# Two steps of a gated recurrence read their input products from a shared block instead of computing them alone

## The chip, the cores and the metric

The kernel runs on one core of one Trainium2 chip. The metric is device time of the whole program in microseconds (us), the median of several executions. One execution was recorded by the hardware profiler; every duration below comes from that record, and times "at 838.95" are us from the start of its span.

## What is computed

Two layers with residual connections over x of 64 sequences x 128 steps x 512 features, all in fp32. The first layer is a gated linear recurrence that the kernel does with scans along time. The second is a GRU whose gates also see a conditioning vector. Cut to the second layer:

```
x  = x + layer0(x, cond)                    # scans, no step-by-step matmuls
xz, xr, xh = x @ W_z, x @ W_r, x @ W        # "products of x", 512 -> 3 x 512
vz, vr, vh = cond @ C_z + b_z, cond @ C_r + b_r, cond @ C + b
for t in range(128):                        # h: 64 x 512
    z  = sigmoid(xz[t] + h @ U_z + vz)
    r  = sigmoid(xr[t] + h @ U_r + vr)
    hh = tanh(xh[t] + (r * h) @ U + vh)
    h  = (1 - z) * h + z * hh
out = x + h of every step
```

## The kernel before

**Two halves of the program.** From the start to about 708 us the first layer runs, in 16 groups of 4 sequences. From there the GRU runs. Only the GRU is touched by the change.

**Two streams.** The 64 sequences are split into stream 0 and stream 1 of 32 sequences each. Their steps alternate on the engines, so that one stream's matmuls run while the other stream's vector work is done. Stream 0 starts four steps earlier; stream 1 takes two steps in a row at three places (`CATCH_UP`, line 1099). Below, s0 t10 is step 10 of stream 0. The list `order` fixes the turns; turn 7 is s1 t0, turn 8 is s0 t4, turn 17 is s0 t8, turn 19 is s0 t9, turn 20 is s1 t7, turn 21 is s0 t10, turn 22 is s1 t8, turn 23 is s0 t11, turn 27 is s0 t13.

**One step on the engines** (`Stream.halves`). TensorE (PE) takes 16 matmuls of 256 columns, the r and z gates, h times U (the group `g<-w_s,h`, line 374). ScalarE (ACT) takes the sigmoid of r (L815) and of z (L824). VectorE (DVE) multiplies r and h and transposes the result in two halves (L819, L820). PE takes 16 matmuls of 128 columns with it (`g<-w_s,f`). ACT takes the tanh (L854), DVE makes the new h and transposes it (L866, L867, L871). GpSimd (POOL) makes (1-z)h (L830, L831) and adds x to the output (L882). [...]

**Where the products of x come from.** They must stand in the PSUM bank `g` of the stream before the step's gates are added to it. There are two ways.

- *Direct.* For steps for which `direct` (line 730) is true, ACT copies the conditioning part into the bank (`put_v`, line 777) and PE adds 16 matmuls of 384 columns (`x_products`, the group `g<-w_x,x`). They are issued as filler in the next turn, between that turn's gates and its second matmul. Before the change stream 0 does so up to step 11, stream 1 up to step 7.
- *Shared.* Steps are also put in groups of 8 (a group covers steps 8g to 8g+7 of both streams). The products of a whole group are made by a two-level fast matrix multiplication (7 outer x 7 inner = 49 products, class `Outer`), each product 4 matmuls of 384 columns (line 500). Group 0 is not made so; group 1 covers steps 8 to 15, for all 64 sequences. Sums of the left operands are made on POOL (L708), copies between banks on ACT (L513, L524), reads into the accumulators on DVE (L597, L602), two further adds on DVE (L617) and POOL (L622). A finished block of two steps goes to DRAM (L630, `shares<-W`); a stream loads the rows of its step (`load_share`, L761) into a tile `xz` if the step is even, and into the tile `whole_v`, which held the conditioning part, if it is odd. ACT puts them in the bank (`put_share`, L767) in place of `put_v`.

A block of steps 8 to 11 is finished by the outer product number 5 of the group (after 35 of its 49 products), a block of steps 12 to 15 by the last ones. `load_share` asserts that the stores of its rows have been issued.

**The pace of the products.** `GOALS` (line 1107) is a list of points (turn, number of products placed); `goal` (line 1112) interpolates between them, and each turn calls `place` twice, after its gates and after its second matmul. `place` (line 714) issues products until the number is reached, but it stops when the next product needs a bank copy from a product of the same outer product that it has issued in the same call. So an outer product's seven products go out over three or four calls, and three calls bring seven products at most. Every product is followed by its reads on DVE and by sums on POOL in program order. All matmuls are issued in the order in which the program writes them.

Of the kernel before, what the change touches and what calls it, by code (L numbers as in the profile page):

```python
# [18 lines left out]
def kernel(  # L19
# [39 lines left out]
    B, S, D = x.shape  # L59
# [5 lines left out]
    TW = 8  # L65
# [298 lines left out]
    NX = S // TW  # L364
# [364 lines left out]

    def direct(st, t):  # L730

        return t < (12 if st.s == 0 else 8)

    class Stream:
        def __init__(self, s):
# [54 lines left out]
        def halves(self, t, filler=None, between=None, targets=lambda: (0, 0), busy=False, reads=(4, 0)):  # L790
# [16 lines left out]
            if t + 1 < S and not direct(self, t + 1) and t + 1 not in self.shares:  # L807
                self.load_share(t + 1)
# [46 lines left out]
            if t + 1 < S and not direct(self, t + 1):  # L855
                self.put_share(t + 1)
# [44 lines left out]
            if t + 2 < S and not direct(self, t + 2) and all((t + 2, q) in stored for q in range(Q)):  # L901
                self.load_share(t + 2)
# [182 lines left out]
    for n in range(2):  # L1085
        t = work.tile([P, 5, 3, P], F32, tag="xt", bufs=2, name=f"w_inner{n}")
# [14 lines left out]
    for t in range(LEAD + 1, S):  # L1101
# [3 lines left out]
    at_of = {step_: FIRST + n for n, step_ in enumerate(order)}  # L1105

    GOALS = (
        (8, 0), (17, 35), (27, 81), (at_of[0, S - TW] - 7, 7 * 7 * (NX - 1) - 14),
        (at_of[0, S - TH] - 5, 7 * 7 * (NX - 1)),
    )  # L1110

# [106 lines left out]
```

## Time and profile before

| what | us |
|---|---|
| median of 3 runs | 1927.61 (1926.23 to 1927.84) |
| the profiled execution | 1927.34 |
| its span on the core | 1925.6 |
| PE busy in the span | 1903.3 |
| DVE, POOL, ACT busy | 1547.2, 838.9, 683.9 |
| `g<-w_x,x`, 640 matmul records (20 blocks of 32) | 55.4 |
| end of the last `g<-w_x,x` block | 855 |
| mean granted PE clock | 0.999 |

A busy time is the union of an engine's instructions; PE instructions overlap in the pipeline, so a block of matmuls is timed here from its first start to the next block's first start. "Idle before" is the time in which an engine stood still ahead of a group, and the arrow names the instruction whose end released it. A chain of waits follows the last instruction back through what released it.

### The profile page before, as it was taken

To read this page: it belongs to the slowest core of one execution; us is meant where nothing else is said; L and a number is where in the kernel's file an instruction comes from. 1 tells how busy PE (TensorE), PEld (TensorE's weight loads), DVE (VectorE), ACT (ScalarE), POOL (GpSimd) and SP (SyncE) were. 2 spreads that over 40 slices of the span, in tenths; PEclk is the share of its full clock that TensorE was granted. 3 is DMA by queue.
4 is the path that set the end of the run, shared out by engine and by line. 5 is a ranking of instruction groups with operands and counts; after the bars stand their busy time and mean duration, and the time that the engine had idled before them with its cause. 6 is when DMAs were issued, how large, how long until landed. Compare 5 with 4: busy or idle time off the path is not lost.

```text
span 1925.6 us, 62747 instructions
## 1 busy us (share of the span) xinstructions
PE 1903.3 (99%) x25225; PEld 1107.7 (58%) x25225; DVE 1547.2 (80%) x3382; ACT 683.9 (36%) x1880; POOL 838.9 (44%) x1542
## 2 busy tenths in 40 slices
PE   9999999999999999999999999999999999999998
PEld 5444444444444445666666666666666666666667
DVE  6899999999999996557777777777777777777776
ACT  3122221212122113234444444444444444444434
POOL 1222223222222325345565655655665655655650
PEclk9999999999999999999999999999999999999999
DMA  6642222222222231233343443443443443443343
GB/s 170 162 93 50 49 44 45 60 49 50 54 47 52 38 66 46 53 95 98 107 133 99 119 130 104 116 131 100 126 122 108 124 122 102 134 117 101 113 110 76
DMA packets 276899, 178.90 MB, mean 93 GB/s; under 512 B 159028, under 2 KB 254528, under 8 KB 276608
## 3 DMA queue, kind: packets, MB, share of 16 engines
q1 hardware_dynamic: 276104, 174.81, 35.6%
q8 instruction: 199, 3.26, 0.7%
q14 instruction: 92, 0.75, 0.1%
q10 hardware_dynamic: 504, 0.07, 0.0%
HBM read 93.58 MB, written 81.13 MB: 91 GB/s over the span
## 4 chain that ended last, share of the span: by engine, by line
PE 65%; DVE 32%; issue 2%; DMA 1%; ACT 0%; POOL 0%; DVEq 0%; ACTq 0%; SPq 0%; POOLq 0%
PE g L374 35%; PE r L500 14%; DVE h L268 10%; PE p L189 4%; DVE h L317 4%; DVE i L300 4%; PE r12a L500 4%; PE shared L500 3%; PE r12b L500 3%; DVE h L307 3%; DVE i L299 2%; DVE i L312 2%; DVE f L284 2%; DVE i L287 2%; DVE h L267 2%
## 5 line engine op out<-in xcount | busy, mean ns | idle before, releaser
L189 PE MATMUL p<-xT,W 128*128 128x512 f32 (+1 forms) x1560 | 670.1, 586 | 1.8 <-ACT xT L148 1.7
L189 PEld LDWEIGHTS p<-xT,W 128*128 128x128 f32 x1560 | 289.6, 190 | 344.2 <-issue 335.9
L374 PE MATMUL g<-w_s,h 128*32 128x256 f32 (+1 forms) x8128 | 481.7, 373 | 3.8 <-DVE h L871 2.1
L374 PEld LDWEIGHTS g<-w_s,h 128*32 128x32 f32 x8128 | 312.6, 110 | 168.3 <-issue 79.0
L374 PEld LDWEIGHTS g<-w_s,f 128*32 128x32 f32 x8128 | 224.5, 109 | 113.2 <-issue 52.1
L374 PE MATMUL g<-w_s,f 128*32 128x128 f32 x8128 | 276.3, 273 | 6.7 <-DVE f L819 5.4
L819 DVE TENSOR_TENSOR f<-f,h 128x64 f32<-128x64 f32 (+1 forms) x494 | 110.7, 224 | 190.5 <-ACT f L815 189.9
L272 POOL COPY first<-condT 128x4 f32<-128x4 f32 x64 | 12.3, 192 | 515.6 <-DVE h L267 501.0
L882 POOL TENSOR_TENSOR h<-h,x 128x128 f32<-128x128 f32 x242 | 123.5, 510 | 237.5 <-DVE h L871 223.5
L268 DVE RECIPROCAL h<-h 128x517 f32<-128x517 f32 x64 | 217.0, 3391 | 2.2
L286 ACT ACTIVATE f<-f 128x512 f32<-128x512 f32 x64 | 40.4, 631 | 461.9 <-DVE f L284 461.9
L815 ACT ACTIVATE f<-g 128x128 f32<-128x128 f32 x254 | 70.6, 278 | 330.7 <-PE g L374 314.4
L830 POOL TENSOR_SCALAR f<-f 128x128 f32<-128x128 f32 x240 | 72.6, 302 | 255.6 <-DVE f L819 248.0
L602 DVE TENSOR_TENSOR W<-r,W 128x384 f32<-128x384 f32 x315 | 170.1, 540 | 9.8 <-PE r L500 0.6
L854 ACT ACTIVATE h<-g 128x128 f32<-128x128 f32 x256 | 71.2, 278 | 242.8 <-PE g L374 242.8
L820 DVE STREAM_TRANSPOSE f<-f 128x64 f32<-128x64 f32 (+1 forms) x494 | 122.2, 247 | 22.5
L866 DVE TENSOR_TENSOR h<-h,f 128x128 f32<-128x128 f32 (+1 forms) x264 | 82.4, 312 | 61.1 <-ACT h L854 61.0
L831 POOL TENSOR_TENSOR f<-f,h 128x128 f32<-128x128 f32 x240 | 112.2, 467 | 20.0
L867 DVE TENSOR_TENSOR h<-h,f 128x128 f32<-128x128 f32 (+1 forms) x264 | 91.9, 348 | 25.8
L210 POOL TENSOR_TENSOR x<-xT,h 128x512 f32<-128x512 f32 x63 | 95.9, 1523 | 4.9
L300 DVE TENSOR_TENSOR_SCAN i<-i,f 128x517 f32<-128x517 f32 x64 | 79.1, 1236 | 6.9 <-ACT i L247 0.5
L317 DVE TENSOR_TENSOR_SCAN h<-f,first 128x517 f32<-128x517 f32 x64 | 79.1, 1236 | 6.5
(167 smaller groups left out, 2790.6 us busy)
## 6 DMA issues: line engine op xcount, KB each, us to landing
shares<-W SPq DMA_DIRECT2D x240, 192.0 KB, 2.0
xz<-shares SPq DMA_DIRECT2D x472, 48.0 KB, 1.9
whole_v<-shares SPq DMA_DIRECT2D x472, 48.0 KB, 1.9
x<-in_x_dram SPq DMA_DIRECT2D x64, 256.0 KB, 4.2
x2d<-x SPq DMA_DIRECT2D x63, 256.0 KB, 3.6
out_dram<-o SPq DMA_DIRECT2D x240, 64.0 KB, 1.8
xw_None<-x2d SPq DMA_DIRECT2D x56, 256.0 KB, 3.4
w_rows<-in_L_cond_W_f_dram SPq DMA_DIRECT2D x4, 256.0 KB, 5.4
```

The source lines that it names most:

```text
L189: nc.tensor.matmul(p[:, tokens], lhsT=W0[:, c, n, k, :], rhs=xT[g][:, k, tokens], start=(k == 0), stop=(k == K - 1),)
L210: nc.gpsimd.tensor_tensor(x2.rearrange("p (t b) -> p t b", b=GB)[:, ts], xT[g][:, c, :].rearrange("p (t b) -> p t b", b=GB)[:, ts], by_bat ...
L268: pin(nc.vector.reciprocal(h, h))
L300: pin(nc.vector.tensor_tensor_scan(i, i, f, 0.0, ALU.add, ALU.mult))
L317: pin(nc.vector.tensor_tensor_scan(h, fs[c % 2], first, 0.0, ALU.mult, ALU.add))
L374: nc.tensor.matmul(p[q * SB : (q + 1) * SB], lhsT=lhsT(k), rhs=part(wk, q), start=(start and k == 0), stop=(stop and k == len(w) - 1), ski ...
L500: nc.tensor.matmul(self.bank(bank)[q * SB : (q + 1) * SB], lhsT=a[:, q * SB : (q + 1) * SB], rhs=w_, start=start, stop=True, skip_group_ch ...
L602: pin(nc.vector.tensor_tensor(dst, r, other, ALU.add))
L819: pin(nc.vector.tensor_tensor(rh[:, e], r[:, e], h_[:, e], ALU.mult))
L820: pin(nc.vector.transpose(rhT[:, e], rh[:, e]))
L831: pin(nc.gpsimd.tensor_tensor(r, r, h_, ALU.mult))
L882: nc.gpsimd.tensor_tensor(hh.rearrange("p (k b) -> p k b", b=SB), hT.rearrange("p (k b) -> p k b", b=SB), x_of(self, t), ALU.add,)
```

## The change

`direct` becomes false for s0 t10 and s0 t11. Stream 0 then computes the products of x by themselves up to step 9, and loads steps 10 and 11 from the shared block. The second point of `GOALS` asks for all 49 products of group 1 by turn 17, where it asked for 35. The third point (81 products by turn 27) and the later ones stay.

```diff
     def direct(st, t):
 
-        return t < (12 if st.s == 0 else 8)
+        return t < (10 if st.s == 0 else 8)
...
     GOALS = (
-        (8, 0), (17, 35), (27, 81), (at_of[0, S - TW] - 7, 7 * 7 * (NX - 1) - 14),
+        (8, 0), (17, 49), (27, 81), (at_of[0, S - TW] - 7, 7 * 7 * (NX - 1) - 14),
         (at_of[0, S - TH] - 5, 7 * 7 * (NX - 1)),
     )
```

## The prediction

> **What bounds the kernel now.** I read the page first for the busiest engine, then the busy times by stage of the GRU, then the timeline of PE around the two blocks that go. The page's first line of engines, the stages (columns: stretch, length, then busy time of PE, PEld, DVE, ACT and POOL, granted clock, DMA share, GB/s) and PE from 837 to 857 us:
>
> ```profile
> PE 1903.3 (99%) x25225; PEld 1107.7 (58%) x25225; DVE 1547.2 (80%) x3382; ACT 683.9 (36%) x1880; POOL 838.9 (44%) x1542
> ```
>
> ```profile
> 736.00:846.00 110.00, 109.86 (x1808) 65.67 (x1812) 62.85 (x177) 36.24 (x112) 45.08 (x90) 1.00 0.24 63
> 846.00:915.00 69.00, 69.00 (x1272) 43.82 (x1268) 50.38 (x152) 30.53 (x92) 39.06 (x79) 1.00 0.35 100
> 915.00:1000.00 85.00, 83.24 (x1596) 53.66 (x1592) 63.03 (x196) 36.84 (x111) 49.05 (x100) 1.00 0.43 118
> 1000.00:1400.00 400.00, 400.00 (x7720) 259.03 (x7714) 297.34 (x948) 180.71 (x543) 230.70 (x480) 1.00 0.42 116
> ```
>
> ```profile
> 838.95 2.79 PE L374 MATMUL g<-w_x,x 128*32 128x384 f32 x32
> 841.53 1.08 PE L374 MATMUL g<-w_s,f 128*32 128x128 f32 x32
> 842.40 0.86 PE L500 MATMUL r12b<-w_inner,inner_sum 128*32 128x384 f32 x8
> 843.05 0.86 PE L500 MATMUL r<-w_x,x 128*32 128x384 f32 x8
> 843.69 1.94 PE L374 MATMUL g<-w_s,h 128*32 128x256 f32 x32
> ...
> 852.54 2.79 PE L374 MATMUL g<-w_x,x 128*32 128x384 f32 x32
> 855.12 1.08 PE L374 MATMUL g<-w_s,f 128*32 128x128 f32 x32
> ```
>
> The reader is to see that PE has no idle time between 736 and 915 us but 0.14 us, while DVE has 57% and 73% of those stretches and POOL 41% and 57%; and that no PE row carries a wait in brackets. A busy PE could hide small gaps, since a block's modelled end overlaps the next block's start by about 0.21 us. So I checked by starts: a block of x products costs 841.53 - 838.95 = 2.58 us, a gates block (h) 845.42 - 843.69 = 1.73, an f block 842.40 - 841.53 = 0.87, a two-level product 843.05 - 842.40 = 0.645. Laying PE's blocks end to end with these four numbers from s0 t4 (742.17) gives the start of s0 t15's gates at 898.72, and the timeline has 898.72. There is not one gap of 0.1 us in 156 us. PE's own work sets the time here, and from 1000 on the stage shows the same.
>
> **The change, part by part.**
>
> *Removed.* The x products of s0 t10 (838.95) and s0 t11 (852.54): 2 x 16 matmuls, 2 x 2.58 = 5.16 us of PE. Both lie in the gapless stretch, so nothing of them is beside other work of PE.
>
> *Kept.* All 49 products of group 1 are made for 64 sequences whether or not stream 0 uses them, so the shared way costs PE nothing more. ACT's copy into the bank is 0.48 us either way (L777 at 848.16 and L767 at 862.39): 0. In the instruction order of the changed kernel, 81 products are placed ahead of s0 t13 as before, and from about there on the order is the same on all five queues but for tile numbers.
>
> *Moved.* The two goals together let products run at the most that the copy rule allows, 7 in three calls, until turn 18. Laid end to end with the same four numbers, the changed order gives:
>
> | start of gates | before | changed | difference |
> |---|---|---|---|
> | s0 t5 | 757.69 | 758.33 | +0.64 |
> | s0 t7 | 796.49 | 799.07 | +2.58 |
> | s0 t9 | 827.53 | 832.04 | +4.51 |
> | s0 t10 | 843.69 | 845.63 | +1.94 |
> | s0 t11 | 857.28 | 856.63 | -0.65 |
> | s0 t13 | 879.93 | 874.77 | -5.16 |
>
> Product 35 starts 5.2 us sooner (805.54 for 810.72), product 49 6.9 sooner (830.11 for 837.02, so in turn 18 and not by 17). A moved product takes along its DVE reads (0.56 each), its ACT copies (0.46 to 0.51) and POOL sums (0.46, or two of 0.72 for an outer sum). A turn in this phase lasts 7.8 to 8.4 us where x products are in it; DVE's busiest such turn before, with the weight differences in it, is 6.7 us (749.93 to 757.69). The changed order there is the same; its fullest later turn, s0 t8, has seven reads and adds of about 0.55 beside the step's own 2.1, so 6.0 of 8.4. I take 0, with 0.5 (one read in the way) as the upper end. No product overtakes a weight difference that it needs: the last one is made at 789.62 before, and product 49, the only one to use it, starts at 830.11.
>
> *Shorter cover.* Where an x block stood between a turn's gates and its f block, only products stand there now. Six turns (s0 t10 to s1 t10) get two products, 1.29 us; before, three of these had that. What must fit in: sigmoid, multiply, transpose. At s1 t9 before, gates' issue ended at 864.83, the first transposed half was ready at 865.97 (DVE L820 ends: 865.73 + 0.25) and the second at 866.37; f started at 866.12, without a gap, since the second half is first needed 0.43 later. So 1.29 is just enough with DVE free. The one visible gap in the run before, at 901.83 after two products, is 0.1. Nearest row for six such turns: 6 x 0.1 = 0.6 at most, likely 0.1. The other end is when POOL works beside DVE; s1 t8 before, from the timeline:
>
> ```profile
> 851.48 1.42 POOL L708 TENSOR_TENSOR sum<-x,sum 128x256 f32<-128x256 f32 x2
> ...
> 851.88 0.41 DVE L819 TENSOR_TENSOR f<-f,h 128x64 f32<-128x64 f32 x1 [1.56 <-ACT f L815]
> 852.33 0.25 DVE L820 STREAM_TRANSPOSE f<-f 128x64 f32<-128x64 f32 x1
> 852.50 0.49 DVE L819 TENSOR_TENSOR f<-f,h 128x64 f32<-128x64 f32 x1
> ```
>
> The multiplies take 0.41 and 0.49 here, beside 0.23 and 0.18 at s1 t9. The second half is ready at 853.27, 2.02 us after the gates' issue: with two products as cover f would be up to 0.73 us late. Here an x block hid it, and the change takes this block away. In the changed order these POOL sums fall in s0 t9 (still with an x block) and s1 t7 (three products), so I take 0.1 and keep 6 x 0.73 = 4.4 as the far end. The Trainium skill (GPSIMD Engine Reference, section Specifications) says that GpSimd's SBUF interfaces are shared with VectorE and contend with instructions of two SBUF inputs, as the multiply is; the two rows above agree. By that rule denser sums speak against the change: stretched at every one of the six turns, the sum would be -0.8 instead of -5.1 (the rival "cover" below).
>
> *Added: eight loads and a wait.* SyncE (SP) issues 4 loads for t10 and 4 for t11, about 0.45 us each (four took 1.79 at 851.90), 3.6 us on a queue that is idle for most of 797 to 862. ACT's `put_share` now waits for them, and behind it stand the next turn's copies and sigmoids, so all of PE. Its due time by the table: the tanh of s0 t9 starts 0.27 after the f block's issue (842.67 against 842.40 before) and the copy 0.31 later, so 838.51 + 0.58 = 839.1. When do the rows come? In the changed order the last two loads of t10 stand behind nine stores on SP, the eighth of which waits for POOL's first late add (L622), in s0 t8. At s0 t9 before, that add ended 5.3 us after the gates' start (832.8 against 827.53); so about 815.23 + 5.3 = 820.5, plus 2.0 for the stores and 1.9 for the loads to land (the page's medians), plus four issues, 1.8: 826.2. That is 12.9 us to spare. In the run before, the analogous load for s1 t8 was issued at 821.80 and used at 842.98:
>
> ```profile
> 821.80 0.31 SPq L761 DMA_DIRECT2D xz<-shares  x1
> ```
>
> ```profile
> 842.98 0.48 ACT L767 COPY g<-xz 128x384 f32<-128x384 f32 x1
> ```
>
> t11 is due about 850 and its last load stands behind the fourth late DVE add or POOL's second add, a turn later (about 835 landed). The tile `xz` for t12 is freed by `put_share` of s1 t8 at about 845 and due at about 861. Cost 0.
>
> *What is late next.* The next wait on the chain is at 919.17, 1.37 us before s1's second step in a row, for DVE (L871). It hangs on that turn's own f block, not on a clock of its own, so it moves along and stays.
>
> **Sum.** -5.16 + 0.1 = -5.1 on the profiled execution's own 1927.34 us: 1922.2. The median before is 0.27 above this execution, so 1922.5 for a median. That is 0.26% faster; a change of under 0.2% (3.9 us) can hardly be told from none here.
>
> **The rivals.**
>
> - *As summed*: 1922.5, between 1921.7 and 1923.7 (0 to 1.1 us given back, by 0.5 of DVE and 0.6 of covers, and the spread of the runs before). For it: the gapless tally. Chance 74%.
> - *Cover*: the shorter covers and denser POOL and DVE work open gaps on PE, 1.2 to 4.4 us in all: 1923.7 to 1926.9. For it: the stretched multiplies. Against: 1000 to 1400 runs at 4.5 us a turn on such covers with PE at 400.00 of 400.00. 12%.
> - *Late rows, slower*: the loads of t10 come behind a later add than I read. In the run before, POOL's four adds end a turn apart, 823 to 848, about 8.2 us each. Behind the fourth and not the first, the rows would land at 826.2 + 3 x 8.2 = 850.8, 11.7 us after 839.1; net +6.6, so 1934.2. It takes time from a landing after 839.1, and loses on balance from 844.2. Against: the order on SP. 5%.
> - *Nothing*: a wait after 877 that does not hang on PE takes up the gain: 1927.6. For it: the rows of later groups also pass DRAM. Against: their stores wait for reads of PE's products, so they move along. 4%.
> - *More*: the wait of 1.37 us at 919 goes as well, because DVE has less left over there: -6.5, 1921.1. 5%.
>
> **How the numbers follow.** The likeliest is 1922.5. The range goes from *more* (1921.1) up into the middle of *cover*, 1925.2; left out are the upper part of *cover*, *late rows* and *nothing*, together some 14%. Faster by over 0.2% (below 1923.75): nearly all of *as summed* and *more*, 0.77. Within 0.2%: *cover*, *nothing* and the edge of *as summed*, 0.18. Slower: 0.05.
>
> **What would show it.** In the changed profile: 576 records of `g<-w_x,x` instead of 640, the last ones in s1 t7; gates of s0 t9 about 4.5 us later and of s0 t13 5.2 us earlier than before; no bracketed wait of PE between 736 and 910; L767 for t10 about 839 right behind its tanh; and the wait of 1.4 us at about 914. A PE gap ahead of `g<-w_s,f` between 845 and 880 would show *cover*; ACT waiting at L767 for `xz<-shares` near 839 or 850 would show *late rows*. The forecast is wrong if some other engine's backlog after 840 reaches PE, which the busy shares do not exclude turn by turn.

## The result, and the profile after

The changed kernel takes **1919.99 us**, the median of 8 executions (1918.50 to 1921.87), against 1926.38 for the kernel before, the median of 8 (1924.65 to 1927.84), the three known before the prediction among them. The ratio is 0.9971, 95% interval 0.9961 to 0.9981: faster by 0.29%. A second comparison, on another occasion, gave 1922.83 (1920.59 to 1924.18, 7 executions) against 1926.90 (23 executions): 0.9975, interval 0.9964 to 0.9987. The forecast was 1922.5 on a level of 1927.61, a ratio of 0.9974. So the forecast ratio lies in both intervals; the absolute number was 2.5 us too high for the first comparison and 0.3 too low for the second, and the first lies below the low end of the range, 1921.1. The profiled execution took 1920.00 us, its span is 1918.0.

The page's first line of engines, then the stages of the GRU (the same columns as for before; the limits are shifted by what PE gained):

```profile
PE 1897.5 (99%) x25161; PEld 1100.3 (57%) x25161; DVE 1544.2 (81%) x3382; ACT 683.5 (36%) x1880; POOL 837.4 (44%) x1542
```

```profile
736.00:846.00 110.00, 109.79 (x1800) 59.45 (x1796) 65.07 (x179) 37.05 (x112) 49.35 (x96) 1.00 0.25 68
846.00:908.00 62.00, 61.95 (x1184) 39.77 (x1180) 46.66 (x146) 28.41 (x86) 32.98 (x71) 1.00 0.37 106
908.00:995.00 87.00, 85.27 (x1634) 55.25 (x1628) 63.79 (x199) 37.56 (x114) 50.65 (x104) 1.00 0.42 115
995.00:1395.00 400.00, 400.00 (x7724) 261.44 (x7717) 296.14 (x948) 180.73 (x543) 230.04 (x480) 1.00 0.42 116
```

PE has 64 instructions less (25225 - 25161), the two x blocks of 32 records (16 matmuls each, and every matmul stands in the trace as two records), and is busy 5.8 us less. Of `g<-w_x,x` 576 records are left, as forecast. It is still the engine that is full in every stage; DVE and POOL do the same number of instructions as before. PE's timeline from the last x block on:

```profile
835.17 2.76 PE L374 MATMUL g<-w_x,x 128*32 128x384 f32 x32
837.75 1.06 PE L374 MATMUL g<-w_s,f 128*32 128x128 f32 x32
...
843.57 1.06 PE L374 MATMUL g<-w_s,f 128*32 128x128 f32 x32
844.45 0.83 PE L500 MATMUL r12a<-w_inner,inner_sum 128*32 128x384 f32 x8
845.09 0.83 PE L500 MATMUL r<-w_x,x 128*32 128x384 f32 x8
845.74 1.91 PE L374 MATMUL g<-w_s,h 128*32 128x256 f32 x32
847.46 0.83 PE L500 MATMUL r<-w_inner,inner_sum 128*32 128x384 f32 x8
848.11 0.83 PE L500 MATMUL r12a<-w_x,inner_sum 128*32 128x384 f32 x8
848.99 1.08 PE L374 MATMUL g<-w_s,f 128*32 128x128 f32 x32
```

The block at 835.17 is the last, for s1 t7; the two of s0 t10 and t11 are gone. The reader should check the starts as the prediction did: each block begins where the tally puts it, but for the last row: 848.11 + 0.645 = 848.755, and the f block starts at 848.99. That is a gap of 0.23 us that no bracket shows. Elsewhere one bracket has come in that before did not have; all of PE's waits from 736 to 1000 (columns: us in total, times, longest):

```profile
PE g L374 <- DVE f L819: 2.6, 2, 2.2
PE g L374 <- DVE h L871: 1.4, 1, 1.4
PE r L500 <- ACT r L513: 0.2, 1, 0.2
```

The first row is the wait ahead of 736 and one of 0.4 at 963, the second the wait at 914; both are in before too. The third is new. The timeline of all engines around it (other rows left out):

```profile
779.74 0.25 DVE L820 STREAM_TRANSPOSE f<-f 128x64 f32<-128x64 f32 x1
779.75 1.08 PE L374 MATMUL g<-w_s,f 128*32 128x128 f32 x32
...
779.90 0.52 DVE L602 TENSOR_TENSOR W<-r,W 128x384 f32<-128x384 f32 x1
...
780.53 0.46 ACT L513 COPY r<-r 128x384 f32<-128x384 f32 x1 [0.94 <-DVE W L602]
...
781.05 0.85 PE L500 MATMUL r<-i,sum 128*32 128x384 f32 x8 [0.21 <-ACT r L513]
```

PE could have gone on at 779.75 + 0.87 = 780.62 and went on at 781.05, 0.43 us later. It waited for ACT's copy, and the copy for DVE's read, which came behind DVE's two transposed halves. A gap of 0.43 by starts shows as 0.21 in brackets, because the modelled end of a block overlaps the next.

### The profile page after: what moved, and what is told of

It reads as the page before. It is cut to its first block, busy times and chain, and to the rows that moved or that the text cites. A ratio compares the mean times of both kernels' runs of the same rounds, so it can differ in the third digit from the quotient of the medians.

```text
span 1918.0 us, 62630 instructions
## 1 busy us (share of the span) xinstructions
PE 1897.5 (99%) x25161; PEld 1100.3 (57%) x25161; DVE 1544.2 (81%) x3382; ACT 683.5 (36%) x1880; POOL 837.4 (44%) x1542
## 4 chain that ended last, share of the span: by engine, by line
PE 81%; DVE 17%; issue 1%; ACT 0%; POOL 0%; DMA 0%; ACTq 0%; DVEq 0%; SPq 0%; POOLq 0%
PE g L374 35%; PE p L189 19%; PE r L500 14%; DVE h L268 5%; PE r12a L500 3%; PE shared L500 3%; PE r12b L500 3%; DVE h L317 2%; DVE i L300 2%; DVE h L307 2%; DVE i L312 1%; PE tp L147 1%; DVE i L299 1%; DVE f L284 1%; DVE i L287 1%
## 5 line engine op out<-in xcount | busy, mean ns | idle before, releaser
L882 POOL TENSOR_TENSOR h<-h,x 128x128 f32<-128x128 f32 x242 | 122.4, 506 | 231.8 <-DVE h L871 219.7
```

Source lines behind the costliest of these rows:

```text
L882: nc.gpsimd.tensor_tensor(hh.rearrange("p (k b) -> p k b", b=SB), hT.rearrange("p (k b) -> p k b", b=SB), x_of(self, t), ALU.add,)
```

## The experiments

All executions of a kernel run the same program, so two records can be laid over each other: I take the start of every f block in one minus its start in the profile of before. To leave out what was lost or won ahead of 736, the shift at 736 is subtracted, and so is one loss of 1.69 us that has a cause of its own (below). The table has this shift at two places, and the difference of the medians of the same comparison.

| kernel | x blocks against before | shift at 883 | shift at 1881 | median, difference |
|---|---|---|---|---|
| before, again | 0 | 0.00 | 0.00 | -0.8 |
| goals alone | 0 | +0.44 | +0.81 | +0.9 |
| direct to step 10, new goal | -1 | -2.13 | -2.40 | -2.4 |
| two blocks put back | 0 | +0.45 | 0.00 | -0.1 |
| two blocks more, old goals | +2 | +5.16 | +4.88 | +3.9 |
| changed | -2 | -4.48 | -5.04 | -6.4 |
| changed, again | -2 | -4.48 | -4.93 | -4.1 |
| changed, goal 45 | -2 | -4.48 | -4.05 | -4.4 |
| direct to step 8 | -3 | -7.07 | -7.03 | -6.5 |
| changed, wait filled | -2 | -4.49 | -4.96 | -7.2 |
| direct to step 8, wait filled | -3 | -7.06 | -7.04 | -7.5 |

**The kernel before, again.** No edit.

> The kernel before, once more, under another name. It tells how far two executions of one program differ, and where. Theory A (the change itself is worth 5.16 us of PE less 0.65 us of new gaps, so 4.5; what the two profiles show beyond that, 0.3 us before 736 us and some 2.4 us after 960 us, is chance of single executions): ratio 1.000 within 0.1%, and a profile whose last 40 us (from s0 t121 on) differ from those of the first profile by something like 1 to 2 us though nothing is changed. Rival B (the extra 2 us at the end come with the change): the last 40 us are as in the first profile within 0.3 us.

1925.57 (1924.15 to 1927.91, 11 executions) against 1926.34 (33 executions, 1924.01 to 1930.70): 0.9999, 0.9990 to 1.0008. Laid over the first record it agrees to 0.07 us at every f block up to 1881, but for one step of 1.69 us between 736 and 764; only the last 45 us differ, by 0.2 to 0.7 us either way at the f blocks and by 1.3 us to the end of the span. So theory A holds: the trace can tell some 0.1 us of a change up to 1881, which the medians can't, and two of these 11 executions lie 3.8 us apart. The level of before is 1926.3 to 1926.9, not the 1927.61 of three executions.

**The goals alone.**

```diff
-        (8, 0), (17, 35), (27, 81), ...
+        (8, 0), (17, 49), (27, 81), ...
```

> The 49 of the second goal alone: s0 t10 and t11 still compute their products of x. PE has the same blocks as before in another order. Theory A: no gain, 1926 within 1.5 us (ratio 1.000); gates of s0 t10 are 4.5 to 5 us late and s0 t13 is at the time of before plus at most 0.7 us, with the small gap near 781 us (a bank copy that waits for a DVE read) as in the changed kernel. Rival (the sooner products are themselves worth something, since PE is fed better): 2 us or more faster.

1927.19 (11 executions), ratio 1.0005, 0.9996 to 1.0014. No gain: placing the products sooner wins nothing by itself. The trace shows the 0.43 us gap (here at 783.26) as a shift of +0.44, so the gap belongs to the goal and not to the blocks. The opposite, the blocks left out with the old goal, has no run: at that pace the stores of the rows of s0 t10 are not yet issued when `load_share` asks for them.

**One block.**

```diff
-        return t < (12 if st.s == 0 else 8)
+        return t < (11 if st.s == 0 else 8)
```

with the new goal.

> Half of the removal: goal 49, s0 t11 from the shared block, s0 t10 still direct, so one block of x products less and not two. Theory A: half of 5.16, less the same gap: 1926.4 - 2.58 + 0.4 = 1924.2, ratio 0.9989. Rival (the gain is not PE time but a matter of phase or of waits): no proportion to the number of blocks, either nothing or the whole 6 us.

1923.93 (11 executions), 0.9987, 0.9979 to 0.9996; the shift is -2.13 = -2.58 + 0.45. One block brings one block's time, less the gap of the goal. The size rests on the shift: the spans of the same executions, without the time outside of them, differ by 3.4 us in the median (1921.1 against 1924.5), so that the medians' 2.4 is near 2.13 in part by chance.

**The two blocks put back.** The changed kernel, with two blocks of the same size and at the same places whose left operand is zeros; they add nothing to the banks.

```diff
+        elif st.s == 0 and ts + 1 < 12:
+            pending.append(
+                lambda: matmuls(
+                    st.g, lambda _: zeros, [w_x[:, k] for k in range(K)], start=False, stop=False
+                )
+            )
```

> The changed kernel with the two blocks put back as 2 x 16 matmuls of 384 columns of zeros against the same weights, at the same places, added into the same bank (they add nothing). Loads, stores, waits and goals are those of the changed kernel. Theory A: PE's 5.16 us come back and nothing else: 1920.0 + 5.2 to 1920.0 + 5.0 (the gap of 0.23 us at 849 closes, as the block covers it), so 1925.1, ratio 0.9993 to 1.000. Rival (the gain comes from what the steps no longer wait for on ACT or DVE): stays near 1921.

1926.25 (11 executions), 1.0002, 0.9993 to 1.0010. PE in this kernel's timeline:

```profile
843.33 2.76 PE L374 MATMUL g<-w_x,zeros 128*32 128x384 f32 x32
...
849.80 0.83 PE L500 MATMUL r<-w_inner,inner_sum 128*32 128x384 f32 x8
850.45 0.83 PE L500 MATMUL r12a<-w_x,inner_sum 128*32 128x384 f32 x8
851.09 1.06 PE L374 MATMUL g<-w_s,f 128*32 128x128 f32 x32
```

Everything else of the change is in, loads and stores included, and all of the gain is gone: it is PE's time of the two blocks. The last rows also show the f block of s0 t10 without its 0.23 us gap (850.45 + 0.645 = 851.09), so that gap needs the blocks to be gone.

**The changed kernel, again.**

> The changed kernel itself, once more. Theory A (PE loses two x blocks, 5.16 us, and 0.65 us come back as two gaps of PE; the rest of the first result, some 1.9 us, is spread between executions: half clock for 3.5 us near 736 in some, and the last turns): ratio to the kernel before 0.9977 (-4.5 us), at most 0.0005 off, and -4.5 also between executions of equal clock. Rival B (the change also shortens the last turns): the ratio stays at 0.9967 to 0.9971, the last 21 turns take 67.8 us again beside 68.9 in the two profiles of before, and executions of equal clock differ by 5.7 or more.

0.9975, near theory A. The last 21 turns took 68.15 us, between the two figures and nearer to rival B's. At a mean granted clock of 1.000 the medians are 1921.13 (2 executions) and 1925.61 (8), 4.5 us apart, on theory A's side, though two executions are few; the two of the first eight at 1.000 took 1919.6, some 6 us less than the kernel before at 1.000 on other occasions, on rival B's side. Rival B's cause does not fit the records: from the f block at 1881 to the end of the span the twelve take 41.3 to 44.6 us, in no order of their x blocks (44.5 and 43.2 before, 42.3 and 42.9 changed, but also 42.8 with two blocks put back and 42.3 with two more). With the loss of 1.69 us taken out, the two records of the changed kernel agree to 0.01 us up to 883 and to 0.1 up to 1881; in the last 45 us they differ by up to 0.6.

**A third block.** In the kernel changed further, s0 t9 is loaded too. For this the late adds of DVE are taken up to four in a step, and the stores go out ahead of the loads:

```diff
-        return t < (10 if st.s == 0 else 8)
+        return t < (9 if st.s == 0 else 8)
...
-            if t + 1 < S and not direct(self, t + 1) and t + 1 not in self.shares:
-                self.load_share(t + 1)
             while to_store:
                 to_store.pop(0)()
+            if t + 1 < S and not direct(self, t + 1) and t + 1 not in self.shares:
+                self.load_share(t + 1)
...
-            add_c()
+            for _ in range(4 if t < 9 else 1):
+                add_c()
```

> As changed, but also s0 t9 reads the shared block (one more x block less), with the adds for steps 8 to 11 taken in one turn so that its rows can be stored and loaded in time. Theory A (each x block is worth its 2.58 us while its rows come in time): 2.3 to 2.6 us below the changed kernel, ratio about 0.9959. Rival, late rows: the rows are due at about 823.0 (0.58 behind the end of the f block of s0 t8 at 822.4) and the last add they need ends at about 816 to 821; landed some 5 us later, they hold ACT's copy and PE for up to 4 us, so that the kernel is 0 to 1.5 us slower than the changed one, ratio 0.9971 to 0.9985, and L767 or L772 waits for shares near 823.

1920.42 (5 executions), 0.9965, 0.9953 to 0.9978, 2.4 us below the changed kernel of the same comparison; the shift is -7.07, 2.59 more. The queue of SP, then ACT:

```profile
811.07 1.79 SPq L761 DMA_DIRECT2D whole_v<-shares  x4
```

```profile
824.90 0.28 ACT L854 ACTIVATE h<-g 128x128 f32<-128x128 f32 x1 [3.64 <-PE g L374]
825.21 0.48 ACT L767 COPY g<-whole_v 128x384 f32<-128x384 f32 x1
```

The four loads for t9 are issued by 812.9 and the copy runs 0.31 behind its tanh, with no wait for a DMA. With the 1.9 us to landing that is some 10 us to spare. Late rows are refuted even for a step earlier, with the adds and stores taken sooner as here.

**A slower goal.**

```diff
-        (8, 0), (17, 49), (27, 81), ...
+        (8, 0), (17, 45), (27, 81), ...
```

> As changed, but with the goal at 45 products by turn 17 instead of 49. Theory A (the 0.43 us gap at 781 comes from products packed closer than ACT's copies and DVE's reads can follow): 0.2 to 0.6 us below the changed kernel, the wait of a product for L513 near 781 gone, ratio 0.0001 to 0.0003 lower. Rival (the limit of seven products in three calls, not the goal, sets the packing there): no difference, the wait still there.

1922.47 (11 executions), 0.9979, 0.9970 to 0.9988: no better. The wait for L513 is still there, at 781.47, and 0.42 us more are lost between 883 and 922. The rival holds as far as the goal goes: 45 packs the products no looser near 781 than 49, where the 35 of before had no such wait. That the limit of seven in three calls sets the packing there follows from the order in the kernel; no run changes that limit.

**Two blocks more.** In the kernel before, goals untouched:

```diff
-        return t < (12 if st.s == 0 else 8)
+        return t < (14 if st.s == 0 else 8)
```

> The kernel before with two x blocks more: stream 0 computes the products of steps 12 and 13 by themselves too; goals as before. Theory A (an x block costs PE's 2.58 us wherever PE has no gap): +5.16 us, less up to 0.2, ratio 1.0026 to 1.0027. Rival (the goals are half of the gain, so blocks alone are worth less): +2 to +3 us, ratio 1.0010 to 1.0016.

The shift is +5.16 at 883, exactly two blocks. The medians say 1930.77 (11 executions), 1.0020, 1.0012 to 1.0029; theory A's 1.0027 is inside, the rival's 1.0016 too, and only the trace decides between them.

**The loss of 1.69 us.** Five of the ten records without an edit at that place have it, five do not, both the changed kernel and the one before in either group. The clock falls to 0.50 for 3.41 us right behind PE's wait of 2.2 us for DVE, ahead of the f block of s0 t3. The record of before, again, at PE:

```profile
735.70 1.49 PE L374 MATMUL g<-w_s,f 128*32 128x128 f32 x32 [2.20 <-DVE f L819]
736.89 6.74 PE L374 MATMUL g<-w_x,x 128*32 128x384 f32 x64
```

The two x blocks take 6.74 us there and 5.37 in the first profile of before.

Why only in five? The traces hold every change of the granted clock with its time. In the twelve records it falls 17 times, five times here and twelve times behind the last matmul, and each fall lies a whole multiple of 3.413 us behind the record's first clock entry, the 214th multiple here. In the five records with the loss the whole wait, 2.2 us, lies in the 3.41 us ahead of that multiple, and PE is busy for 1.22 to 1.24 us of them. In the other five a multiple cuts the wait: 1.43 to 1.90 us of it lie in these 3.41 us, and PE is busy for 1.51 to 1.99. The stretch and the one behind it in the record of before, again, then the same stretch in the first profile of before (columns as above; granted clock third from the end):

```profile
732.81:736.23 3.42, 1.22 (x36) 0.69 (x28) 1.79 (x5) 2.16 (x10) 2.56 (x4) 1.00 0.06 9
736.23:739.64 3.41, 3.41 (x41) 1.94 (x36) 1.21 (x4) 1.63 (x6) 0.89 (x2) 0.50 0.73 152
```

```profile
732.28:735.69 3.41, 1.67 (x32) 0.76 (x24) 1.01 (x1) 1.33 (x7) 3.05 (x4) 1.00 0.04 5
```

The Trainium skill (TensorE: Matmul & The Clock Gate, section "What's actually happening") has the clock halved after an idle window of about 3.4 us whose phase is free, which would differ from execution to execution. The trace agrees on the half clock, on its length and on the free phase; but here PE is busy for 1.2 us of the stretch, so a single wait of 3.4 us isn't needed. The wait of 0.9 us that the expectation below adds to it ends at 728.99, ahead of the stretch, and plays no part in this reading. To test it, 12 matmuls of zeros into banks that hold zeros were put into the wait:

```diff
     next(step_3)
+    for block in ((0, 1, 0), (1, 0), (1, 1)):
+        matmuls(banks[block], lambda _: zeros, [w_s[:, 0]])
```

> The changed kernel with 12 matmuls of zeros (into banks that hold zeros already; no result uses them) in PE's wait of 2.2 us ahead of the f block of s0 t3, at 733.5 to 735.7. Five of ten profiled executions run at half the granted clock for 3.5 us right behind this wait, which costs 1.7 us. Theory A (the wait, with the 0.9 us one before it, is what lowers the clock): no half clock near 736 to 740, mean clock 1.000 in most executions, and a median 0.5 to 1.0 us below that of the changed kernel, ratio to the kernel before 0.9968 to 0.9973. Rival B (the clock falls there whatever PE does in the wait): half clock in about half of the executions as before, ratio 0.9973 to 0.9977.

1919.42 (5 executions), 0.9964, 0.9952 to 0.9977, and with the third block as well:

> Both at once: s0 t9 from the shared block too (one more x block less), and the 12 matmuls of zeros in the wait. Theory A: the two add up, 2.3 to 2.6 us and 0.5 to 1.0 us below the changed kernel, ratio 0.9956 to 0.9962. Rival B: only the block counts, ratio 0.9960 to 0.9966.

1919.13 (5 executions), 0.9958, 0.9944 to 0.9972, the fastest ratio of all. PE in the record of the first of the two:

```profile
734.69 1.47 PE L374 MATMUL r<-w_s,zeros 128*32 128x384 f32 x16
736.47 1.08 PE L374 MATMUL g<-w_s,f 128*32 128x128 f32 x32 [0.30 <-DVE f L819]
737.34 5.37 PE L374 MATMUL g<-w_x,x 128*32 128x384 f32 x64
```

A wait of 0.30 is left, the x blocks take 5.37, and the clock is 1.00. Nine of these ten executions have a mean granted clock of 1.000, against 20 of 65 of the kernel before. A fall of 3.41 us to half takes the mean to 0.9991, so 1.000 rules it out; the tenth execution is the profiled one of the first run, and its only fall lies behind the last matmul. So the wait is what lowers the clock, and in ten of ten records its place against the multiples of 3.413 us tells whether it does. Where between 1.24 and 1.51 us of busy time the limit lies was not tested. That the medians fall by the 0.5 to 1.0 us that follows from it is not shown: the interval of the ratio is wider than that, though both medians lie below those without the filling.

## Why the prediction was right and its number was not

**Removed, -5.16: right.** The shift at 883 is -4.48 = -5.16 + 0.43 + 0.23 to 0.02 us. One block fewer gives -2.58 with the gap of the goal added, three fewer -7.74 with both gaps, two more +5.16, and two put back give all of it away.

**Moved work at 0, upper end 0.5: the upper end.** The gates of s0 t9 start at 832.15 and those of s0 t13 at 875.11. The changed record is 0.34 us ahead at 736 already; without that, they are 4.96 us later than before where the table had 4.51, and 4.48 sooner where it had 5.16. The wait at 781 lies ahead of both, where no bracketed wait was forecast. The prediction set DVE's busy time against a turn's length, 6.7 of 7.8 us; what counted was the order inside a turn: DVE's read stood behind the multiplies, ACT's copy behind the read, PE's product behind the copy, and PE had only an f block, 0.87, in between.

**Shorter covers at 0.1: undersized, but one turn only.** At the first of the six turns the multiply is stretched. DVE in the changed kernel's timeline, then POOL:

```profile
848.02 0.46 POOL L882 TENSOR_TENSOR h<-h,x 128x128 f32<-128x128 f32 x1
...
848.08 0.48 DVE L819 TENSOR_TENSOR f<-f,h 128x64 f32<-128x64 f32 x1 [0.45 <-ACT f L815]
...
848.76 0.18 DVE L819 TENSOR_TENSOR f<-f,h 128x64 f32<-128x64 f32 x1
```

It takes 0.48 beside POOL's add, its second half 0.18 once that has ended, and the f block is 0.23 late. In this record none of the 391 such multiplies that ran with POOL idle took more than 0.23. The prediction had looked for POOL's sums at these turns; what stood here is its add of x to the output (L882). The far end, 4.4 at six turns, was far off, and too high by the prediction's own reading: the second half is first needed 0.43 after the f block's start, so the row of s1 t8 gives 0.30 late and not 0.73, 1.8 at six turns. The rival *cover* explains 0.66 us together with the moved work, less than the 1.2 at which it begins.

**Loads and the wait: right.** The last two loads of t10 are issued from 822.17 to 823.75 and so land near 825.6, where 826.2 was forecast. L767 runs behind its tanh at 839.18 (forecast 839.1) and 850.43 (about 850), with no wait. *Late rows* is refuted, and again by the third block.

**What is late next: right.** PE's wait for L871 is 1.35 us at 914.33 (forecast 1.4 at about 914). *More* rested on its going and is refuted, though the first time came out below *More*'s 1921.1; a number may agree with a case whose mechanism is not there. *Nothing* is refuted by the shift, which is -4.98 on average at 1881.

**The sum.** By 1881 the changed kernel is 5.04 and 4.93 ahead in its two records, where -5.1 was forecast: 0.66 given back around 781 and 849, and some 0.5 more won, of which about 0.2 between 1000 and 1005. Where that comes from was not followed up.

**What failed** is the step from there to the time: "The median before is 0.27 above this execution, so 1922.5 for a median", and with it the range of *as summed*, 1921.7 to 1923.7, by "the spread of the runs before". Three executions gave a level of 1927.61 and a spread of 1.6. More of them give 1926.38 (8, those three among them), 1926.34 (33) and 1926.90 (23), and single executions go from 1924.0 to 1930.7. So some 1.2 us of the 2.5 is the level. The other 1.3 is that the first 8 executions of the changed kernel gained 6.4 and the next 7 gained 4.1, about a gain of 5 in the middle. Two parts of this spread have a cause in the traces. One is the 1.69 us of half clock in some executions and not in others. The other is in the last 75 us, which took 76.08 and 74.82 us in two records of before and 73.93 and 74.51 in two of the changed kernel. The first of these, the very record that the forecast started from, has a wait that the other three lack: in its chain of waits a load into `xz` takes 3.62 us from 1905.99 on, where the page's median from issue to landing is 1.9, and holds ACT and PE:

```profile
1909.71 0.38 ACT L772 COPY g<-xz 128x256 f32<-128x256 f32 x1 [1.68 <-DMA xz<-shares]
```

```profile
1910.14 1.08 PE L374 MATMUL g<-w_s,h 128*32 128x128 f32 x32 [0.68 <-ACT g L772]
```

Across it that record loses 1.0 us on the other one of before and 0.8 on the first of the changed kernel. The longest end of the twelve, 44.6 us from 1881 on (direct to step 8, wait filled), has such waits too, of 1.4 and 0.6 us. Why a load lands late in one execution is open. So is the rest of the last turns, where PE's waits are mostly put down to "issue", at other places in each record, and whether the half clock was rarer in the first 8 executions: their mean clocks (two of eight at 1.000) don't say so. A low end of 1919.5 would have followed from the forecast if the level of before had been given an error of 1.5 us and the median after another 1.5.

## What to carry to other kernels

Where an engine runs without a gap, by starts and not by busy share, a block taken from it is worth its start-to-start time, here 2.58 us each to within 0.02, for one, two or three of them, once the two new gaps are counted; but check the order of the reads and copies inside each turn that gets fuller, not only its sum. A forecast of an absolute time carries the error of the level it starts from: with three executions that was 1.2 us here, a quarter of the whole gain, and the range has to hold it beside the errors of the sum. For changes of this size, lay two records over each other, block by block, before reading medians: that told 0.1 us where the medians told 2.

## What the runs showed of the hardware that was not expected

A wait of 2.2 us on PE halved the granted clock for the next 3.41 us in five of ten records, which cost 1.69 us each time. It did so where the whole wait fell between two neighbouring multiples of 3.413 us from the first clock entry (PE busy for 1.22 to 1.24 us between them), and not where a multiple cut it (1.51 to 1.99); with matmuls of zeros in the wait it did not in two of two. Otherwise two records of one program, of each of the two that have two, repeat to 0.1 us over 1100 us of the GRU, waits included: the differences lie in that one place, ahead of 721 (up to 0.9 us between any two of the records) and in the last 45 us.
